# A transformer block on one core: the feed-forward computed by seven block products

## The chip, the cores and the metric

The kernel runs on one core of one Trainium2 chip. A core has five engines that work side by side, each through its own queue of instructions: TensorE (PE in the profile: matrix products, with the loading of the stationary operand shown apart as PEld), VectorE (DVE), ScalarE (ACT), GpSimd (POOL) and SyncE (SP), which here issues every DMA transfer. The engines work on SBUF, the on-chip memory of 128 partitions, and on PSUM, where products accumulate. Large data lie in DRAM and are moved by 16 DMA engines. The metric is the device time of one execution in microseconds (us). Before the change it is 2405.66 us, the median of three runs (2404.91 to 2408.99).

## The reference

One transformer block over 4096 tokens of 512 features, in fp32: linear attention, then a feed-forward, each added to its input and followed by a normalisation (eps 1e-5).

```python
x = layernorm(x + attention(x, Wq, Wk, Wv, Wo))
x = layernorm(x + ffn(x, ...))

# attention: 16 query heads, 4 key/value heads, 128 features each
q, k = elu(rope(q)) + 1, elu(rope(k)) + 1
state += k_s (x) v_s;  z += k_s                # running sums over the tokens s
out_s = (q_s . state) / (q_s . z + 1e-6)       # then out @ Wo.T

# ffn: 512 -> 2 x 2048 -> 512; fwht is the normalised Walsh-Hadamard transform
u = fwht(x * SU_ug) / 64
h = silu(u @ W_gate.T * (Wscale_ug[2048:] * 64)) * (u @ W_up.T * (Wscale_ug[:2048] * 64))
y = (fwht(h * SU_dp) / 64) @ W_down.T * (Wscale_dp * 64)
```

## The kernel before

**Precision.** Every fp32 operand of a product is split into two fp32r numbers: `hilo` (L89) copies the value to fp32r on ACT (L90), and DVE, or POOL where it is told so, subtracts the copy from the value (L91). Each product is then three matmuls: high by high, high by low and low by high.

**Attention** (L134 to L488, 0 to 941 us) runs in two halves of the heads over 16 blocks of 256 tokens: projections (`proj`, L239, 256 columns), the rotary part (POOL L221), scores, running states. It writes the unnormalised outputs to `num_d` and the reciprocals of the denominators to `rec_d`. The change leaves it as it is.

**Output projection** (L540 to L645). 32 tiles of 128 tokens. `pre` (L118) loads a tile's numerators `nt` (1 MB), its reciprocals `rb` (four loads of 256 KB, broadcast over the partitions) and its residual `xn`. `norm_o` (L549) multiplies the two on DVE (L552), one group of four heads at a time, and splits the result. 48 matmuls of 128x512 (L622) make the tile's projection in `ps_wo`; DVE adds the residual (L627), `layer_norm` (L530) takes statistics, an inverse square root of small operations (`rsqrt_small`, L32, L35 to L43) and the normalisation (L538) on DVE, and the tile goes to `y_d`.

Two more things run beside this stage. `prep_down` (L576), started at the tiles in `starts`, folds the second Walsh-Hadamard transform into the down weights: per eighth of the columns, a Hadamard matmul (L589, L590) does 7 of 11 steps, DVE scales (L591), POOL does the other four steps (L598, 64 operations of 128x512), and the split result goes to `wdn_d` in two puts of 512 KB, in runs of 256 bytes. `front` (L495) makes the first block's feed-forward input: sign product (L504), nine add/subtract steps (L509, L510), four transposes (L518) and a split; for block 0 it runs on POOL.

**Feed-forward** (L648 to L715, 1316.6 to the end). Eight blocks of 512 tokens. In each, 16 iterations `it` over 128 rows of the up and gate weights: `load_wug` (L522) loads and splits the weights, 2 x 12 matmuls of 128x512 (L682) fill `ps_gu`, ACT takes silu (L687), DVE multiplies (L688), and the product is split into `hh_h` and `hh_l`, which stay in SBUF for the block. The fronts of the next block run among the iterations, alternately on DVE and POOL. Then four tiles of 48 down matmuls (L707) with the down weights kept in SBUF since block 0, the residual (L713), the second norm and the store.

**Order.** The program is written as one sequence. A scheduler that simulates the timeline places the instructions on the engines; each engine then works through its queue in order. All DMA issues stand in SP's one queue, so a transfer that waits for data holds back the issues behind it; the transfers rotate over eight completion semaphores. A tile pool gives a buffer out again when its last reader is done.

Of the kernel before, what the change touches and what calls it, by code (L numbers as in the profile page):

```python
# [9 lines left out]
F32 = mybir.dt.float32  # L10
# [11 lines left out]
TF = 512  # L22
NF = NTOK // TF
EPS_DEN = 1e-6
EPS_LN = 1e-5
# [6 lines left out]
def rsqrt_small(nc, pool, v, tag):  # L32
    y = pool.tile([128, 1], F32, tag=tag + "y", name=tag + "y")
    a = pool.tile([128, 1], F32, tag=tag + "a", name=tag + "a")
# [3 lines left out]
    for _ in range(3):  # L38
        nc.vector.tensor_scalar(a, y, y, v, ALU.mult, ALU.mult)
        nc.vector.scalar_tensor_tensor(y, a, c, y, ALU.subtract, ALU.mult)  # L40
        f = f * -0.5 if c == 3.0 else f / (-2.0 * c / 3.0)
        c = 3.0 / (f * f)
# [5 lines left out]
def kernel(  # L48
# [28 lines left out]
    wdn_d = dram.tile([16, 128, 2, 512], F32, name="wdn_d")  # L77
# [39 lines left out]

    def pre(t):  # L118
        if t in (12, 16):
            recip(NB - 2 + (t == 16))  # L120
        nt = late["p"].tile([128, 16, 128], F32, tag="nt", name="nt", bufs=3)
        if t:
            dma(nt, num_d[t].rearrange("p g n -> p (g n)"), t < 3)
        rb = []
        for g in range(4):
            if t == 0:
                dma(nt[:, 4 * g:4 * g + 4], num_d[t][:, g])
            rb.append(late["p"].tile([128, 512], F32, tag="rb", name="rb", bufs=5))
            dma(rb[g], rec_d[t][g * 512:(g + 1) * 512].partition_broadcast(128), 0 < t < 3 and g == 0)
        xn = late["p"].tile([128, DM], F32, tag="xn", name="xn")  # L130
        dma(xn, x_n[t * 128:(t + 1) * 128])
        cur[t] = dict(nt=nt, rb=rb, xn=xn)

# [357 lines left out]
    suug = mid.tile([128, DM], F32, name="suug")  # L491
    wsc = mid.tile([128, 2, 16], F32, name="wsc")
    Y, YT = {}, {}

    def front(pool, fpool, nb, ptr, f, t, eng):  # L495
        if t == 0:
            Y[f] = []
        y = pool.tile([128, DM], F32, tag="y", name="y")
        dma(y, y_d[4 * f + t])
        Y[f].append(y)  # L500
        yield
        a = fpool.tile([128, DM], F32, tag="fw0v" if eng is V else "fw0g", name="fw0", bufs=1)
        b = fpool.tile([128, DM], F32, tag="fw1", name="fw1", bufs=nb)
        eng.tensor_tensor(a, y, suug, ALU.mult)  # L504
        w = 1
        while w < DM:
            aa = a.rearrange("p (n r w) -> p n r w", r=2, w=w)
            bb = b.rearrange("p (n r w) -> p n r w", r=2, w=w)
            eng.tensor_tensor(bb[:, :, 0], aa[:, :, 0], aa[:, :, 1], ALU.add)  # L509
            eng.tensor_tensor(bb[:, :, 1], aa[:, :, 0], aa[:, :, 1], ALU.subtract)  # L510
            a, b = b, a
            w *= 2
        yield
        if t == 0:
            YT[f] = tuple(mid.tile([128, 4, TF], F32R, tag="yT", name=n, bufs=2) for n in ("yTh", "yTl"))
        ps = ptr.tile([128, 4, 128], F32, tag="tr", name="ps_tr")
        for k in range(4):
            T.transpose(ps[:, k], a[:, k * 128:(k + 1) * 128], idt)  # L518
        h, l = (z[:, :, t * 128:(t + 1) * 128] for z in YT[f])
        hilo(h, l, ps)  # L520

    def load_wug(it):  # L522
        w = mid.tile([128, 2, 2, 4, 128], F32R, tag="wug", name="wug_s", bufs=2)
        wf = w.rearrange("p l u k m -> p l (u k m)")
        for j in range(2):
            c = slice(j * 512, (j + 1) * 512)
            hilo(wf[:, 0, c], wf[:, 1, c], load_raw(wug[it, :, c]))
        return w

    def layer_norm(pool, x, o, tag):  # L530
        bs = pool.tile([128, 6], F32, tag="bs", name="bs")
        mv = pool.tile([128, 2], F32, tag="mv", name="mv")
        vv = pool.tile([128, 1], F32, tag="vv", name="vv")
        V.bn_stats(bs, x)
        V.bn_aggr(mv, bs)
        V.tensor_scalar(vv, mv[:, 1:2], EPS_LN, None, ALU.add)
        rs = rsqrt_small(nc, pool, vv, tag)
        V.tensor_scalar(o, x, mv[:, 0:1], rs, ALU.subtract, ALU.mult)  # L538

# [1 line left out]
    with ExitStack() as es:  # L541
        p2 = es.enter_context(tc.tile_pool(name="c2", bufs=2, reuse_waits="tile"))
        p1 = es.enter_context(tc.tile_pool(name="c1", bufs=1, reuse_waits="tile"))
        pwo = es.enter_context(tc.tile_pool(name="pwo", bufs=3, space=PSUM, reuse_waits="tile"))
        pfd = es.enter_context(tc.tile_pool(name="pfd", bufs=2, space=PSUM, reuse_waits="tile"))
        ptc = es.enter_context(tc.tile_pool(name="ptc", bufs=1, space=PSUM, reuse_waits="tile"))
        pon = es.enter_context(tc.tile_pool(name="pon", bufs=2, space=PSUM, reuse_waits="tile"))

        def norm_o(t, g):  # L549
            c = cur[t]  # L550
            o32 = pon.tile([128, 4, 128], F32, tag="on", name="ps_on")
            V.tensor_tensor(o32, c["nt"][:, 4 * g:4 * g + 4], c["rb"][g].rearrange("p (h n) -> p h n", h=4), ALU.mult)  # L552
            hi, lo = (p2.tile([128, 4, 128], F32R, tag="o", name=n, bufs=10) for n in ("oh", "ol"))
# [4 lines left out]
        for h in (NH - 2, NH - 1):  # L558
            WO.append(load_w(wo[h], mid, bufs=4))
# [213 lines left out]
```

## Time and profile before

| What | us |
|---|---|
| Median of three runs (range) | 2405.66 (2404.91 to 2408.99) |
| Profiled execution, span from first to last instruction | 2408.2 |
| Attention, to the first output projection | 0 to 941.3 |
| Output projection | 941.3 to 1316.6 |
| Feed-forward, first block | 1316.6 to 1467.3 |
| Feed-forward, a later block (period) | 133.4 |
| Last operation of the tail begins | 2404.5 |

The profile gives one execution's span (first to last instruction), 2.5 us above the median of the runs. A row of a group or a timeline names start or count, duration, engine, source line, operation, the tiles written and read, and the shape (partitions x elements). Matmuls are pipelined: their shown duration (0.39 us for 512 columns) is longer than the distance from one to the next, so prices of matmuls are taken from stretches of the chain. "Granted clock" is the share of TensorE's full clock that it was given in a stretch.

### The profile page before, as it was taken

The numbers are of one execution on the slowest core, as the hardware profiler recorded it, in microseconds if no ns is written. First come the engines' busy times: TensorE is split into PE (matmuls) and PEld (weight loads), VectorE is DVE, ScalarE is ACT, GpSimd is POOL, SyncE is SP. The second block draws the span as 40 slices with busy tenths as digits, with TensorE's granted clock in tenths as the row PEclk, the third lists the DMA queues.
The fourth block names the chain that finished last, engine by engine and source line by source line (L and its number), as shares of the span: only waits on it lengthen the run. The fifth ranks groups of instructions, "written<-read, shape, count | busy, mean of one in ns | idle before, by whom it ended". The sixth has DMA issues, their size and how long they took to land.

```text
span 2408.2 us, 38221 instructions
## 1 busy us (share of the span) xinstructions
PE 2356.0 (98%) x13600; PEld 2040.2 (85%) x13600; DVE 1825.2 (76%) x3408; ACT 1106.5 (46%) x1928; POOL 848.6 (35%) x839
## 2 busy tenths in 40 slices
PE   7999999999999998999999899999999999999998
PEld 6999999999999996777888688888888888888887
DVE  6999999998888897999998847475655757475443
ACT  5777777777777774222222332314141323324140
POOL 2455454454444452684242504022220405031000
PEclk9999999999999998999999899999999999999999
DMA  6555555644554447878885532213131222223120
GB/s 181 144 157 147 176 145 151 170 132 133 140 146 137 125 135 244 285 235 274 272 275 176 177 131 76 92 60 98 44 114 59 91 70 88 83 70 95 42 92 18
DMA packets 223583, 329.97 MB, mean 137 GB/s; under 512 B 62398, under 2 KB 99328, under 8 KB 219424
## 3 DMA queue, kind: packets, MB, share of 16 engines
q1 hardware_dynamic: 223392, 327.53, 44.6%
q8 instruction: 107, 1.75, 0.3%
q14 instruction: 84, 0.69, 0.1%
HBM read 209.62 MB, written 76.02 MB: 119 GB/s over the span
## 4 chain that ended last, share of the span: by engine, by line
PE 89%; DVE 6%; DMA 2%; issue 2%; ACT 1%; POOL 0%; SPq 0%; DVEq 0%; ACTq 0%; POOLq 0%
PE ps_gu L682 28%; PE ps_qk L239 16%; PE ps_dn L707 15%; PE ps_wo L622 12%; PE ps_num L366 6%; PE ps_s L289 4%; PE ps_v L192 3%; PE ps_sc L332 1%; PE ps_den L367 1%; PE ps_sc L333 1%; DMA rb<-rec_d 1%; DVE ps_on L552 1%; PE ps_tr L518 1%; DVE fw L510 1%; PE pt L277 0%
## 5 line engine op out<-in xcount | busy, mean ns | idle before, releaser
L682 PE MATMUL ps_gu<-yTh,wug_s 128*128 128x512 f32 x2048 | 646.4, 392 | 9.8 <-DVE wug_s L91 4.1
L682 PEld LDWEIGHTS ps_gu<-yTh,wug_s 128*128 128x128 f32 x2048 | 385.8, 189 | 95.3 <-DVE wug_s L91 8.6
L682 PE MATMUL ps_gu<-yTl,wug_s 128*128 128x512 f32 x1024 | 400.6, 391 | 0.0
L239 PE MATMUL ps_qk<-xh,wh 128*128 128x256 f32 x1280 | 358.7, 280 | 5.7 <-ACT wh L90 3.9
L239 PE MATMUL ps_qk<-xl,wh 128*128 128x256 f32 x1280 | 357.0, 279 | 0.6 <-DVE xl L91 0.6
L239 PE MATMUL ps_qk<-xh,wl 128*128 128x256 f32 x1280 | 357.2, 279 | 0.0
L346 POOL TENSOR_SCALAR_AFFINE_SELECT A<-A 64x512 fp32r<-64x512 f32 x256 | 219.9, 859 | 315.5 <-DVE am L342 208.8
L707 PE MATMUL ps_dn<-wdn,hh_h 128*128 128x512 f32 x1024 | 327.9, 396 | 0.0
L688 DVE SCALAR_TENSOR_TENSOR hh<-ps_gu,wsc,sg 128x512 f32<-128x512 f32 x128 | 95.9, 749 | 269.1 <-PE ps_gu L682 267.9
L221 POOL TENSOR_TENSOR sw<-sw,csb 128x512 f32<-128x512 f32 x160 | 217.2, 1358 | 166.8 <-ACT sw L220 158.5
L90 ACT ACTIVATE wug_s<-raw 128x512 fp32r<-128x512 f32 x256 | 150.5, 626 | 230.2 <-PE ps_gu L682 192.9
L239 PEld LDWEIGHTS ps_qk<-xh,wh 128*128 128x128 f32 x1280 | 242.4, 189 | 6.9 <-ACT wh L90 4.1
L504 POOL TENSOR_TENSOR fw<-y,suug 128x512 f32<-128x512 f32 x18 | 25.1, 1393 | 633.2 <-DMA y<-y_d 603.1
L239 PEld LDWEIGHTS ps_qk<-xl,wh 128*128 128x128 f32 x1280 | 241.9, 189 | 1.8 <-DVE xl L91 0.8
L239 PEld LDWEIGHTS ps_qk<-xh,wl 128*128 128x128 f32 x1280 | 241.7, 189 | 1.1
L707 PEld LDWEIGHTS ps_dn<-wdn,hh_h 128*128 128x128 f32 x1024 | 191.6, 188 | 43.7
L682 PEld LDWEIGHTS ps_gu<-yTl,wug_s 128*128 128x128 f32 x1024 | 193.5, 189 | 40.4
L687 ACT ACTIVATE sg<-ps_gu,wsc 128x512 f32<-128x512 f32 x128 | 87.7, 686 | 264.5 <-PE ps_gu L682 264.0
L622 PE MATMUL ps_wo<-wh,ol 128*128 128x512 f32 x512 | 203.9, 398 | 1.7 <-DVE ol L91 1.7
L622 PE MATMUL ps_wo<-wh,oh 128*128 128x512 f32 x512 | 203.3, 397 | 2.2 <-ACT oh L90 2.2
L622 PE MATMUL ps_wo<-wl,oh 128*128 128x512 f32 x512 | 202.8, 396 | 0.0
L707 PE MATMUL ps_dn<-wdn,hh_l 128*128 128x512 f32 x512 | 202.1, 395 | 0.0
(122 smaller groups left out, 5116.3 us busy)
## 6 DMA issues: line engine op xcount, KB each, us to landing
raw<-in_wug_dram SPq DMA_DIRECT2D x256, 256.0 KB
vd<-vhl SPq DMA_DIRECT2D x128, 256.0 KB
num_d<-num SPq DMA_DIRECT2D x128, 256.0 KB
rb<-rec_d SPq DMA_DIRECT2D x128, 256.0 KB
nt<-num_d SPq DMA_DIRECT2D x31, 1024.0 KB
y<-y_d SPq DMA_DIRECT2D x36, 256.0 KB
raw<-in_x_t_dram SPq DMA_DIRECT2D x32, 256.0 KB
csb<-in_cs_dram SPq DMA_DIRECT2D x32, 256.0 KB
```

Source lines behind the costliest of these rows:

```text
L90: S.activation(hi, src, AF.Copy)
L192: T.matmul(ps[:, t], B[xa][:, k, t * 128:(t + 1) * 128], w[:, k % 2], start=i == 0, stop=i == 11)
L221: G.tensor_tensor(sw, sw, sinb, ALU.mult)
L239: T.matmul(ps[:, j], W[key][wa][:, k * 128:(k + 1) * 128], B[xa][:, k], start=i == 0, stop=i == 11)
L289: T.matmul(ps[:, i], B["kfn"][r, g, i // 2], B["vs"][r, i // 2, g * 128:(g + 1) * 128], start=True, stop=True)
L346: G.affine_select(ah, ah.bitcast(F32), pattern=[[0, 8], [1, 64]], compare_op=ALU.is_ge, fill=0.0, base=0, channel_multiplier=-1)
L366: T.matmul(ps[:, c2], l, r, start=i == 0, stop=i == len(ops) - 1)
L622: T.matmul(ps, l[:, h], r, start=i == 0, stop=i == 47)
L682: T.matmul(ps, w[:, wa, u, k], ya[:, k], start=i == 0, stop=i == 11)
L687: S.activation(sg, pu[0], AF.Silu, scale=wsc[:, 1, it:it + 1])
L688: V.scalar_tensor_tensor(hh, pu[1], wsc[:, 0, it:it + 1], sg, ALU.mult, ALU.mult)
L707: T.matmul(ps, l[:, ts], r, start=i == 0, stop=i == 47)
```

## The change

The feed-forward's matrix products are made by a Strassen-Winograd scheme: both operands are cut into 2 x 2 blocks, and the four result blocks come from seven block products of sums and differences of the blocks, instead of eight. `WKEY` names the seven weight operands (A11, A12, A22 and the combinations S1 to S4), `YKEY` the seven token operands (B11, B21, B22 and T1 to T4), and `SEQ` the PSUM bank in which each product is accumulated.

*Gate/up.* Four blocks f of 1024 tokens, each of two halves (even and odd tiles), and eight units p of 2 x 128 rows. A unit has 7 x 2 x 6 matmuls of 128x512. `aload` loads weight blocks of 256 KB; in block 0 `acomb` makes S1 to S4 on POOL and writes them to `was_d`, from where later blocks load them; `asplit` splits every operand of every unit. ACT copies partial sums (`sv`), DVE adds (`cc`), ACT takes silu, POOL (three of four) or DVE multiplies. The four results and POOL's four combinations of them give seven arrays that go to `hop_d` unsplit.

*Token operands.* `front` now works on pairs of tiles: four transposes per tile, the sign product on DVE, a split, a Hadamard matmul pair for seven of the nine transform steps, the other two as additions on DVE and POOL, three more combinations on POOL, and seven puts of 128 KB to `yq_d`, in runs of 512 bytes. Twelve of the sixteen pairs are made in the output projection, four in block 0. `yload` and `ysplit` bring a block's seven operands in.

*Down weights.* `prep_down` makes the seven down operands: the same Hadamard matmuls and POOL steps, 16 POOL combinations more, 28 splits, and 56 puts of 256 KB to `wdop_d`, in runs of 256 bytes (before: 16 puts of 512 KB).

*Down stage.* It stands alone at the end: 8 units x 7 products x 48 matmuls of 128x256. Every step loads its 1 MB operand from `hop_d` in four pieces, two steps ahead, and splits it again (ACT; DVE, or POOL for one or two of four). Results are added to the residual on DVE, then the second norm and the store.

*Output projection.* Two of a tile's four `norm_o` products move from DVE to POOL; the norm works on pairs of tiles, its inverse square root on two columns at once, and the normalisation itself moves from DVE to ACT; the reciprocal loads are issued one group at a time (`pre_rb`); `nt` has two buffers, not three, and the split outputs eight, not ten; the first feed-forward weights are no longer loaded there.

The diff, cut to its core:

```diff
 def rsqrt_small(nc, pool, v, tag):
...
     for _ in range(3):
-        nc.vector.tensor_scalar(a, y, y, v, ALU.mult, ALU.mult)
+        nc.vector.tensor_tensor(a, y, y, ALU.mult)
+        nc.vector.tensor_tensor(a, a, v, ALU.mult)
         nc.vector.scalar_tensor_tensor(y, a, c, y, ALU.subtract, ALU.mult)
...
+    def layer_norm(pool, xs, tag):
...
+        V.scalar_tensor_tensor(nb, mv[:, :, 0], -1.0, rs, ALU.mult, ALU.mult)
+        for j, x in enumerate(xs):
+            S.activation(x, x, AF.Identity, bias=nb[:, j:j + 1], scale=rs[:, j:j + 1])
+
+    SEQ = ("a", "c", "a", "b", "a", "a", "b")
+    WKEY = ("A11", "A12", "S2", "S1", "S3", "A22", "S4")
+    YKEY = ("B11", "B21", "T2", "T1", "T3", "T4", "B22")
+
+    def front(i, y2, spool, ptr, phd, alloc):
...
+        for e in range(2):
...
+                T.transpose(ps[:, k], y2[e][:, k * 128:(k + 1) * 128], idt)
...
+            V.tensor_tensor(ysu, ps, sut[:, :, None].to_broadcast([128, 4, 128]), ALU.mult)
...
+            hilo(hl[:, 0], hl[:, 1], ysu)
...
+            T.matmul(ps, hadr, hl[:, 0], start=True, stop=False)
+            T.matmul(ps, hadr, hl[:, 1], start=False, stop=True)
...
+            S.activation(odd, pa[:, :, 1], AF.Copy)
...
+            V.tensor_tensor(da[:, :, 0], pa[:, :, 0], odd, ALU.add)
+            V.tensor_tensor(da[:, :, 1], pa[:, :, 0], odd, ALU.subtract)
...
+        G.tensor_tensor(q[:, 0], d[:, :, 0:2], d[:, :, 2:4], ALU.add)
+        G.tensor_tensor(q[:, 1], d[:, :, 0:2], d[:, :, 2:4], ALU.subtract)
...
+            dma(yq_d[f][YKEY.index(key)][:, :, c * 128:(c + 1) * 128], x)
...
+        G.tensor_tensor(tt[:, 0], q[:, 0, 1], q[:, 0, 0], ALU.subtract)
+        G.tensor_tensor(tt[:, 1], tt[:, 0], q[:, 1, 1], ALU.subtract)
+        G.tensor_tensor(tt[:, 2], tt[:, 1], q[:, 1, 0], ALU.add)
...
         def norm_o(t, g):
...
+            if g % 2 == 0:
+                o32 = pon.tile([128, 4, 128], F32, tag="on", name="ps_on")
+                V.tensor_tensor(o32, c["nt"][:, 4 * g:4 * g + 4], rb, ALU.mult)
+            else:
+                o32 = p2.tile([128, 4, 128], F32, tag="o32", name="o32")
+                G.tensor_tensor(o32, c["nt"][:, 4 * g:4 * g + 4], rb, ALU.mult)
...
+            for key in ("B11", "B21", "B22", "T3", "T1", "T2", "T4"):
+                if key in fn:
+                    G.tensor_tensor(B[key], *fn[key])
+                x = ytile([128, 2, 8, 64], F32R, "dohl")
+                hilo(x[:, 0], x[:, 1], B[key])
+                for j in range(2):
+                    dma(wdop_d[YKEY.index(key)][j, :, :, qq * 64:(qq + 1) * 64], x[:, j])
...
+        def acomb(n, key):
...
+            G.tensor_tensor(x, r(p0), r(p1), op)
+            RAW[n, key] = x
+            dma(was_d[p][key], x.rearrange("p u k m -> p (u k m)"))
+
+        def asplit(n, s):
...
+            hilo(hi, lo, RAW[n, WKEY[s]])
...
+        for n in range(NS):
...
+            for s, tag in enumerate(SEQ):
...
                 for u in (1, 0):
...
+                    for k in range(2):
+                        for w, y in ((wh, yh), (wh, yl), (wl, yh)):
+                            T.matmul(ps, w[:, u, k], y[:, k], start=first and i == 0, stop=i == 5,
+                                     skip_group_check=not first)
...
+                    if s in (0, 2, 4):
...
+                        S.activation(x, ps, AF.Copy, scale=sc)
...
+                    if s in (1, 4, 6):
...
+                        V.scalar_tensor_tensor(x, src, sc, sv[k, u], ALU.mult, ALU.add)
+                        emit(u, q, x)
...
+                if n + 1 < NS:
+                    aprep(n + 1, s)
+                if n + 2 < NS:
+                    aload(n + 2, s)
...
+            for key, x0, x1, op in (("S1", "A21", "A22", ALU.add), ("S3", "A11", "A21", ALU.subtract),
+                                    ("S2", "S3", "A22", ALU.subtract), ("S4", "A12", "S2", ALU.add)):
+                H[key] = utile("h" + key)
+                G.tensor_tensor(H[key], H[x0], H[x1], op)
+                put(key)
...
+        def h_load(n, s):
...
+            for qd in range(4):
+                raw = pd.tile([128, 2, 256], F32, tag="hr", name="hraw", bufs=8)
+                dma(raw, hop_d[f][s, jp, :, 2 * qd:2 * qd + 2])
...
+        def h_split(n, s):
...
+                hilo(hi, lo, raw, G if qd == 1 or (qd == 3 and s % 2) else V)
...
+        for idx, (n, s) in enumerate(order):
+            if idx + 2 < len(order):
+                h_load(*order[idx + 2])
+            if idx + 1 < len(order):
+                h_split(*order[idx + 1])
...
+            for ip in range(8):
+                qd, r = divmod(ip, 2)
+                for j in range(2):
+                    js = slice(j * 128, (j + 1) * 128)
+                    for al, bl in ((0, 0), (0, 1), (1, 0)):
+                        T.matmul(ps[:, j], ops[qd][al][:, r, js], BW[s][bl][ip], start=first and i == 0, stop=i >= 45,
+                                 skip_group_check=True)
...
+            def acc(y, cols, src):
+                V.tensor_tensor(y[:, :, cols], src, y[:, :, cols], ALU.add)
...
```

## The prediction

> **What bounds the kernel now.** First the busy shares, then the chain of work that ended last:
>
> ```profile
> span 2408.2 us, 38221 instructions
> PE 2356.0 (98%) x13600; PEld 2040.2 (85%) x13600; DVE 1825.2 (76%) x3408; ACT 1106.5 (46%) x1928; POOL 848.6 (35%) x839
> ...
> PE 89%; DVE 6%; DMA 2%; issue 2%; ACT 1%; POOL 0%; SPq 0%; DVEq 0%; ACTq 0%; POOLq 0%
> ```
>
> TensorE (PE) is the bound: 98% busy, 89% of the chain. Fewer matmuls save time only if nothing else takes over, so next I cut the span into stages (columns: stretch, length, busy time of each engine, granted clock, DMA share, GB/s). The rows are attention, output projection, the first feed-forward block, the other seven up to the last down products, and the end; the last two rows are short stretches inside the output projection.
>
> ```profile
> 0.00:941.30 941.30, 910.99 (x7296) 864.26 (x7296) 836.20 (x1394) 688.61 (x1224) 448.45 (x433) 0.99 0.53 150
> 941.30:1316.60 375.30, 370.90 (x1584) 297.67 (x1585) 356.08 (x751) 97.97 (x168) 164.49 (x140) 0.99 0.81 260
> 1316.60:1467.30 150.70, 140.92 (x595) 113.17 (x594) 99.42 (x184) 42.02 (x69) 41.60 (x47) 0.94 0.41 135
> 1467.30:2357.40 890.10, 890.10 (x3944) 730.71 (x3944) 515.94 (x1023) 277.32 (x467) 194.01 (x220) 1.00 0.24 78
> ...
> 1141.00:1165.00 24.00, 24.00 (x107) 19.42 (x107) 23.47 (x60) 7.40 (x13) 1.19 (x1) 1.00 0.86 288
> 1303.00:1305.00 2.00, 2.00 (x10) 1.65 (x9) 1.96 (x8) 0.30 (x1) 0.00 (x0) 1.00 1.04 248
> ```
>
> The feed-forward has room: VectorE (DVE) 58%, GpSimd (POOL) 22%, DMA 24%. The output projection has little: DVE 95%, DMA share 0.81, PE 99%. The change puts new work into the stage with the least room, so that stage decides. Its timeline, POOL and DVE side by side, and one DVE row from the tail, where POOL rests:
>
> ```profile
> 1040.78 3.00 POOL L598 TENSOR_TENSOR dbf<-dbf 128x512 f32<-128x512 f32 x2
> ...
> 1045.12 2.99 POOL L598 TENSOR_TENSOR dbf<-dbf 128x512 f32<-128x512 f32 x2
> ```
>
> ```profile
> 1041.59 0.95 DVE L40 SCALAR_TENSOR_TENSOR r1y<-r1a,r1y 128x1 f32<-128x1 f32 x1
> ...
> 1045.10 1.86 DVE L552 TENSOR_TENSOR ps_on<-nt,rb 128x512 f32<-128x512 f32 x1
> ...
> 2403.13 0.16 DVE L40 SCALAR_TENSOR_TENSOR r2y<-r2a,r2y 128x1 f32<-128x1 f32 x1
> ```
>
> Beside POOL a one-column L40 takes 0.95 us instead of 0.16 and L552 1.86 instead of its fastest 0.68; POOL's L598 has 1.61 as its median and 1.28 as its fastest. Operations of DVE with two SBUF inputs and POOL operations get in each other's way: to first order their times add. L91 from PSUM at 1044.02 kept 0.68.
>
> Matmul prices come from the chain of one block:
>
> ```profile
> 1489.90 10.88 PE ps_gu L682 x48
> ...
> 1586.33 14.40 PE ps_dn L707 x62
> ```
>
> So 0.2267 us per gate/up matmul (512 columns) and 0.2323 per down matmul. In attention, 256-column matmuls come at 4.32 us for 38, 0.1137 each.
>
> **The change part by part.**
>
> *Attention* is not touched: 941.3.
>
> *Gate/up on PE.* 32 units x 7 products x 2 x 6 = 2688 matmuls of 512 columns in place of 3072: 696 becomes 609, 87 saved. All of it lies on the path.
>
> *Down on PE.* 2688 matmuls of 256 columns in place of 1536 of 512. At 0.1137 they take 306; at 0.120 (five 256-column ps_num of attention take 0.60) 323. I take half of 0.2323, since operands come the same way: 312, against 357. 45 saved.
>
> *Output projection.* PE: 1536 x 0.2323 = 357, 80 Hadamard matmuls x 0.23 = 18, 96 transposes x 0.12 = 12 (twelve front pairs; they were spread over the blocks before): 387. With the 4 us idle of now, 391 is the lower end. Hidden behind it must be:
> - POOL: 64 norm_o products moved from DVE, 64 L598 steps as now, 16 new weight combinations, at 1.28 each, and 12 fronts of two 512-column and three 256-column combinations (2x1.28 + 3x0.61 = 4.4): 184 + 53 = 238 us (now 131 by the same prices).
> - DVE with two SBUF inputs: 64 norm_o and 64 splits of POOL's results, 24 + 44 + 14 splits in fronts, weights and token operands, at 0.60 from start to start, 126; 144 small norm operations x 0.2 and some scalings: about 165 in all (now about 130).
> - These add up to 403, more than PE's 387. Now they are about 260 in 375, and the stage still runs at PE's rate.
> - DVE's operations from PSUM (projection adds, 64 splits, statistics, front work) are some 130 more; POOL runs beside those. Moving the normalisation to ACT costs nothing: ACT is 26% busy here.
> - DMA: per tile 2.62 MB (num_d, four rb, x, y_d), 84 MB at 335 GB/s (288 at share 0.86) = 251; 56 new weight puts in 256-byte runs, 14.7 MB at the 241 that 248 at share 1.04 comes to, 61; 84 token puts, 11 MB in 512-byte runs, of which no row exists: 33 to 46, taken 39; reads 24. Sum 375, a share of 0.9.
>
> I take 403 for the shared access plus 9 for the ends of the stage, where one engine waits for another: 412. Upper end: POOL's operations at the contended 1.61, 238x1.61/1.28 = 299, + 165 = 464, + 4 = 468. I stay near the lower end of the sum because 1.61 holds DVE's time already.
>
> The Trainium skill, page "SBUF — State Buffer", section "SBUF: two separate sides", says the shared VectorE/GpSimd port is an exclusive lock, held for the whole instruction; this speaks against moving norm_o to POOL, and this trace agrees (0.16 against 0.95). By the rule alone the stage would be 403; without it, by PE, 391.
>
> The page "DMA: Bandwidth & Descriptors", section "Specifications", wants at least 512 bytes for line rate. The trace has 241 GB/s for 256-byte writes against 335. By the rule the token puts would cost 33 of the bounds above.
>
> *Start of the feed-forward.* The first weight load stands in SP's queue behind the y_d puts of the last tile, which wait for the first norm: about 3.3 for statistics and rsqrt, 1.2 ACT, then load 3, split 1.3 and a POOL combination: 11, with a colder clock 15. The block that starts there now also loses 17 (150.7 against a period of 133.4, whose 1467.30 row runs at clock 1.00).
>
> *Block 0* (8 units). PE has four fronts more: 20.0 per unit. POOL: per unit 4 weight combinations, 3 multiplies, 4 result combinations at 1.29 and 2.2 of front: 16.4; DVE's operations with two SBUF inputs 5.5: 21.9, less a little as fronts leave units free: 21.5, so 172. Ends: 160 (PE) and 208 (16.4x1.61/1.28 + 5.5 = 26).
>
> *Blocks 1 to 3*: no weight combinations; POOL 9 + DVE 5.5 under 19.04 of PE; 24 x 19.04 x 1.02 = 466. Block boundaries with seven token loads and splits: 6. Feed-forward: 15 + 172 + 466 + 6 = 659. DMA moves 14 times 256 KB per unit, 3.7 MB in 19 us or 193 GB/s, against 335.
>
> *From feed-forward to down.* The first loads of the down stage are queued on SP behind the last result puts. After the last matmul: DVE 0.75, POOL multiply 1.3, combinations in series 3.9, put and load 3 each, split 1.3, cold start 1: 14. Now nothing of this exists, since down products run inside each block. Ends: 6 if the weights' order lets PE start early, 20 if put and load both take the 5 us of the y_d load after 1323.
>
> *Down stage.* Each step has 48 matmuls, 5.57 us. ACT four splits and a norm share, 3.2; DVE 3 to 4.5; POOL 2; DMA 1 MB plus residuals, 4. All fit; 6 us for stalls: 318.
>
> *Tail.* Two halves in pairs: 10 against 7.7.
>
> Sum: 941.3 + 412 + 659 + 14 + 318 + 10 = 2354, against the profiled span of 2408.2, which itself lies 2.5 above the median of the runs (2405.66; 2404.91 to 2408.99). Forecast 2352: 132 of matmul time is saved, 78 paid back.
>
> **The rivals.** (1 is the forecast.)
> 2. *All covered*: output projection 391, block 0 160, start 13, boundaries 0, down 306 + 4, transition 6, rest of the blocks 457: 941 + 391 + 630 + 6 + 310 + 10 - 2.5 = 2286. For it: the DVE/POOL sum exceeds PE by 4% only. Against: DVE is 95% busy there already.
> 3. *Down paced by loads*: 1.3 MB per step at 288 GB/s is 4.5, and if the split of 2 follows in series, 6.5 per step, 56 x 0.93 = 52 more: 2404, no change. Against it: two steps are loaded ahead, so load and split overlap.
> 4. *Shared access (slower)*: POOL at its contended price in the output projection, 468, and in block 0, 208: 56 + 36 = 92 more, 2444. For it: DVE loses about 4 of 8.5 us between 1040.5 and 1049 while POOL works without rest. Against: POOL has pauses and DVE's PSUM operations to run beside. It decides from 54 us of that excess on, e.g. POOL operations at about 1.47 in both places.
> 5. *256-column matmuls cost more than half*, say 0.133 as 0.28 us operations that overlap less: down saves nothing, 2398. Against: 38 of them in 4.32.
>
> **How the numbers follow.** Two executions differ by 0.2% at most as a rule, so 2400.8 to 2410.5 counts as the same. Chances: forecast 0.42 (its own range 2318 to 2395), all covered 0.18, down paced by loads 0.08, shared access 0.27, matmul price 0.05. Faster: 0.42 + 0.18 + half of 3 and 5, 0.66; same 0.06; slower 0.28. The range runs from 2286, the covered case, to 2460, the contended one with the upper ends of the down stage (323) and the transition (20) on top (11 + 6); about one in ten is left on each side.
>
> **What would show it.** Right: ps_wo lasts about 412 us with POOL near 60% busy and PE idle behind splits of o; gate/up units every 21.5 us in block 0 and 19.1 later; a single PE gap of 14 before the first down product; down matmuls 0.116 apart. Wrong: POOL's norm_o products or DVE's L40 at several times their free price over the whole stage (case 4); DMA share at 1 with PE waiting for nt or rb; PE waiting for hraw in every step (case 3); a chain of PE alone (case 2).

## The result

The changed kernel takes 2424.91 us (median of four runs, 2419.77 to 2428.04), the kernel before 2405.28 us on the same chip (2404.31 to 2408.99): a ratio of 1.0078, 95% interval 1.006 to 1.0095. It is slower by 0.8%, where 2352 us had been forecast. The page of the changed kernel, busy shares and chain:

```profile
span 2418.0 us, 42274 instructions
...
PE 2281.5 (94%) x14432; PEld 2016.3 (83%) x14432; DVE 1908.3 (79%) x3062; ACT 1354.9 (56%) x2320; POOL 1235.2 (51%) x993
...
PE 74%; DVE 12%; DMA 8%; issue 3%; ACT 2%; POOL 1%; SPq 1%; DVEq 0%; ACTq 0%; POOLq 0%
```

PE has 74 us less to do than before (2281.5 against 2356.0), but its part of the chain fell from 89% to 74%: DVE and DMA now carry a fifth of the span. The profiled execution's span is 2418.0, 6.9 below the median of the runs, so the accounts below are made from profiled execution to profiled execution. By stages (columns as before; the rows are the output projection from its first to its last matmul, the gap to the first gate/up matmul, block 0, most of blocks 1 to 3, the gap ahead of the down stage, the down stage):

```profile
939.30:1373.70 434.40, 404.56 (x1710) 319.12 (x1710) 381.91 (x645) 137.24 (x241) 251.40 (x191) 0.97 0.79 246
1373.70:1393.20 19.50, 1.42 (x4) 0.60 (x3) 13.09 (x24) 5.62 (x7) 10.62 (x8) 0.56 0.50 166
1393.20:1585.20 192.00, 172.22 (x713) 134.53 (x713) 148.87 (x160) 104.97 (x174) 149.11 (x103) 0.96 0.78 244
...
1630.90:2063.00 432.10, 431.65 (x1850) 347.05 (x1848) 277.69 (x311) 228.65 (x375) 234.95 (x156) 1.00 0.67 212
2063.00:2085.90 22.90, 0.22 (x2) 0.02 (x1) 0.75 (x1) 0.98 (x3) 6.27 (x5) 0.55 1.04 390
2085.90:2408.50 322.60, 321.71 (x2688) 321.05 (x2688) 209.66 (x468) 158.23 (x251) 106.84 (x80) 0.99 0.68 225
```

| Stretch, us | forecast | measured | difference |
|---|---|---|---|
| start to first gate/up matmul (attention, output projection, gap) | 1368.3 | 1393.2 | +24.9 |
| block 0 | 172 | 192.0 | +20.0 |
| blocks 1 to 3 | 472 | 477.6 | +5.6 |
| gap ahead of down | 14 | 22.9 | +8.9 |
| down stage | 318 | 322.6 | +4.6 |
| tail | 10 | 9.5 | -0.5 |
| sum | 2354 | 2418.0 | +64 |

In the output projection PE is idle for 30 of 434 us, and its own work is slower as well: 404.6 us busy at a granted clock of 0.97, against 391.8 at 0.99 for the same matmuls in run e9 below. What it waits for there and in the gap (waits of PE: what waited, for whom, us in total, times, longest; `yp` is a pair's projection and residual, normalised in place, `woh` the high part of a weight operand, `r1a` a scratch tile of the norm's inverse square root):

```profile
PE ps_tr L539 <- ACT yp L527: 18.4, 8, 3.7
PE ps_a L840 <- ACT woh L93: 11.9, 1, 11.9
PE ps_fd L647 <- DVE r1a L38: 6.2, 1, 6.2
```

Transposes of the fronts stand in PE's queue and wait for the normalised tile. The norm is late because of its small operations. Timeline of the changed kernel, POOL and then DVE, in the last tiles:

```profile
1382.35 2.48 POOL L658 TENSOR_TENSOR dbb<-dba 128x512 f32<-128x512 f32 x2 [26.84 <-DVE r1y L40]
1384.91 5.05 POOL L658 TENSOR_TENSOR dbb<-dbb 128x512 f32<-128x512 f32 x4
```

```profile
1376.04 0.16 DVE L38 TENSOR_TENSOR r1a<-r1y 128x2 f32<-128x2 f32 x1
...
1382.37 1.26 DVE L38 TENSOR_TENSOR r1a<-r1y 128x2 f32<-128x2 f32 x1
1383.66 1.18 DVE L39 TENSOR_TENSOR r1a<-r1a,vv 128x2 f32<-128x2 f32 x1
```

The same two-column operation takes 0.16 us while POOL rests and 1.26 beside it. A norm of a pair has 14 small operations in series, all of them on two columns.

Two prices are also to be seen in the chain, a stretch of gate/up and one of down:

```profile
1706.89 2.33 PE ps_c L840 x10
```

```profile
2127.78 5.71 PE ps_db L953 x48
```

0.2333 us per gate/up matmul where 0.2267 had been taken from the kernel before, 0.119 per down matmul where 0.116 had been.

### The profile page after: what moved, and what is told of

Read it like the earlier page. It is cut to its first block, busy times and chain, and to the rows that moved or that the text cites. A ratio compares the mean times of both kernels' runs of the same rounds, so it can differ in the third digit from the quotient of the medians.

```text
span 2418.0 us, 42274 instructions
## 1 busy us (share of the span) xinstructions
PE 2281.5 (94%) x14432; PEld 2016.3 (83%) x14432; DVE 1908.3 (79%) x3062; ACT 1354.9 (56%) x2320; POOL 1235.2 (51%) x993
## 4 chain that ended last, share of the span: by engine, by line
PE 74%; DVE 12%; DMA 8%; issue 3%; ACT 2%; POOL 1%; SPq 1%; DVEq 0%; ACTq 0%; POOLq 0%
PE ps_qk L248 15%; PE ps_a L840 12%; PE ps_da L953 8%; PE ps_wo L699 7%; PE ps_b L840 6%; PE ps_num L375 5%; PE ps_db L953 4%; PE ps_s L298 4%; PE ps_c L840 3%; PE ps_v L201 3%; PE ps_dc L953 2%; PE ps_sc L341 1%; DVE wol L94 1%; PE ps_sc L342 1%; PE ps_den L376 1%
## 5 line engine op out<-in xcount | busy, mean ns | idle before, releaser
L823 POOL TENSOR_TENSOR cc<-cc 128x512 f32<-128x512 f32 x96 | 147.9, 1542 | 248.9 <-ACT cc L820 141.9
L93 ACT ACTIVATE hah<-hraw 128x512 fp32r<-128x512 f32 x224 | 138.9, 630 | 155.1 <-PE ps_da L953 58.7
L840 PE MATMUL ps_a<-yoh,woh 128*128 128x512 f32 x512 | 203.5, 398 | 18.9 <-ACT woh L93 17.5
L94 DVE TENSOR_TENSOR wol<-S,woh 128x512 fp32r<-128x512 f32 x128 | 144.5, 1132 | 92.6 <-ACT woh L93 77.0
L94 POOL TENSOR_TENSOR hal<-hraw,hah 128x512 fp32r<-128x512 f32 x80 | 106.8, 1337 | 214.7 <-ACT hah L93 170.7
L840 PE MATMUL ps_a<-yol,woh 128*128 128x512 f32 x512 | 203.4, 397 | 0.0
L840 PE MATMUL ps_a<-yoh,wol 128*128 128x512 f32 x512 | 199.2, 396 | 1.8 <-DVE wol L94 1.8
L94 DVE TENSOR_TENSOR hal<-hraw,hah 128x512 fp32r<-128x512 f32 x144 | 106.7, 747 | 117.8 <-ACT hah L93 108.3
L847 ACT ACTIVATE sv<-ps_a,wsc 128x512 f32<-128x512 f32 x192 | 127.5, 681 | 60.3 <-PE ps_a L840 60.2
L611 POOL TENSOR_TENSOR o<-nt,rb 128x512 f32<-128x512 f32 x64 | 87.2, 1363 | 131.4 <-DVE ol L94 72.5
```

The source lines that it names most:

```text
L93: S.activation(hi, src, AF.Copy)
L94: eng.tensor_tensor(lo, src, hi.bitcast(F32), ALU.subtract)
L823: G.tensor_tensor(x, x, c.pop(("g", q)), ALU.mult)
L840: T.matmul(ps, w[:, u, k], y[:, k], start=first and i == 0, stop=i == 5, skip_group_check=not first)
L847: S.activation(x, ps, AF.Copy, scale=sc)
```

## The experiments

All ratios are to the kernel before, run beside each on the same chip. "First to last ps_wo" is the length of the output projection. A unit, below, is 84 gate/up matmuls, taken from its first matmul to the next unit's first; block 0 has eight.

| Run | median us | ratio (95%) | first to last ps_wo | block 0 |
|---|---|---|---|---|
| changed kernel | 2424.9 | 1.0078 (1.006 to 1.0095) | 434 | 192 |
| e1_norm_dve | 2402.3 | 0.9982 (0.9973 to 0.9991) | 412 | 195 |
| e2_late_fronts | 2419.7 | 1.0059 (1.0044 to 1.0074) | 429 | 194 |
| e3_few_puts | 2417.7 | 1.0051 (1.0036 to 1.0066) | 428 | 192 |
| e4_early_h | 2421.6 | 1.0071 (1.0054 to 1.0088) | 434 | 191 |
| e5_no_comb | 2417.2 | 1.0043 (1.0028 to 1.0058) | 437 | 184 |
| e6_nofwht | 2392.3 | 0.9934 (0.9917 to 0.9952) | 412 | 180 |
| e7_lncols | 2386.2 | 0.9910 (0.9893 to 0.9926) | 395 | 197 |
| e9_lncols_only | 2388.7 | 0.9926 (0.9911 to 0.9940) | 398 | 193 |
| e10_pace | 2401.1 | 0.9976 (0.9966 to 0.9985) | 421 | 181 |
| e11_bw_late | 2398.4 | 0.9965 (0.9953 to 0.9978) | 421 | 181 |
| e13_pad | 2414.7 | 1.0034 (1.0022 to 1.0046) | 434 | 189 |
| e14_before_pad | 2396.7 | 0.9959 (0.9945 to 0.9972) | | |
| e16_best | 2368.1 | 0.9840 (0.9826 to 0.9853) | 392 | 195 |
| e17_best2 | 2354.5 | 0.9778 (0.9765 to 0.9792) | 391 | 195 |

### What holds the output projection: e1, e2, e3

Theory: POOL and DVE hinder each other (shared access). Rivals: the place of the transposes in PE's queue; the DMA traffic of the puts.

```diff
 def norm_o(t, g):                                   # e1_norm_dve
-    if g % 2 == 0:
-        o32 = pon.tile(...); V.tensor_tensor(o32, c["nt"][:, 4 * g:4 * g + 4], rb, ALU.mult)
-    else:
-        o32 = p2.tile(...); G.tensor_tensor(o32, c["nt"][:, 4 * g:4 * g + 4], rb, ALU.mult)
+    o32 = pon.tile(...); V.tensor_tensor(o32, c["nt"][:, 4 * g:4 * g + 4], rb, ALU.mult)
```

> All four norm_o products of a tile go back to DVE (64 operations of 128x512 leave POOL); all else as in the changed kernel. Three theories for the output projection, which lasted 434 us from the first to the last ps_wo where PE's own work is 387. Shared access (POOL operations and DVE operations with two SBUF inputs exclude each other): POOL's share falls by 64 x 1.28 = 82 us, the sum of both from about 403 to 320, so the stage falls to 395 to 410 and the kernel by 25 to 40 us. PE's queue (transposes of the fronts stand ahead of ps_wo and wait for the norm): the waits of ps_tr for yp stay, under 10 us. DMA (the puts delay rb and nt): nothing changes in the traffic, under 5 us.

22 us less in the stage, and the kernel at 2402, 22.6 less. Shared access gave the sign; the size fell just short of it (412 for 395 to 410, 22.6 for 25 to 40), and 412 is still 21 above PE's 391, although the sum of POOL's and DVE's shared work is now 320 by the forecast's prices, far below PE's. The sum is not what sets the stage.

```diff
-        fr.append(wo_front(t // 2, [yp[:, 0], yp[:, 1]]))      # e2_late_fronts
+        fr.append((t, wo_front(t // 2, [yp[:, 0], yp[:, 1]])))
...
-    for x in list(fr):
-        step(x, 3)
+    for t0, x in list(fr):
+        if t - t0 >= 2:
+            step(x, 3)
```

> The fronts in the output projection are started two tiles later, so that their transposes come up in PE's queue about two tiles (25 us) after the last projection matmul of their pair instead of one. PE's queue theory: the waits of ps_tr for yp (18.4 us in eight places, and the colder clock after them) go, the kernel gains 15 to 30 us. Shared access: DVE is as late as before, the idle time of PE turns up as waits for oh and ol, gain under 8 us. DMA: under 5 us.

The waits of ps_tr for yp went, as PE's queue theory said, but waits of the Hadamard matmuls for fhl and others, 24.5 us together, stand in their place, and the stage is 5 us shorter. The place in PE's queue is not the cause: DVE is late, whoever waits for it.

```diff
     for j in range(2):                               # e3_few_puts
-        dma(wdop_d[...][j, ...], x[:, j])
+        if key in ("B11", "B21", "B22"): dma(wdop_d[...][j, ...], x[:, j])
```

> Four of the seven down-weight operands (T1 to T4) are made and split but not written, and the down stage reads B11's in their place: 32 of 56 puts in 256-byte runs are left out, 8.4 MB or some 35 us of DMA time; this part of the result is not computed. DMA theory: loads of rb and nt come earlier, 20 to 35 us gained in the output projection. Shared access and PE's queue: DVE, POOL and PE do the same work, within 8 us of the changed kernel.

The DMA share in the stage fell from 0.79 to 0.73 and its length by 6 us. DMA has a small part at most.

### The norm's small operations: e7, e9

```diff
-    nc.vector.tensor_tensor(a, y, y, ALU.mult)
-    nc.vector.tensor_tensor(a, a, v, ALU.mult)
+    for j in cols:                                   # one column each
+        nc.vector.tensor_scalar(a[:, j], y[:, j], y[:, j], v[:, j], ALU.mult, ALU.mult)
     nc.vector.scalar_tensor_tensor(y, a, c, y, ALU.subtract, ALU.mult)
```

The shift, the last scaling, the eps and the bias are written per column in the same way. e7_lncols is on top of e1, e9_lncols_only on top of the changed kernel.

> On top of e1_norm_dve, the norm's small operations work column by column with scalar operands, as in the kernel before, so that only three of them per pair have two SBUF tensors as inputs (before this edit nine, and the two-column scalings were held up by POOL as well). Shared access says that each held-up operation costs up to 1.2 us of latency: about 8 per pair less, 16 pairs; the norm of a pair is done 5 to 9 us earlier, the waits of ps_tr for yp (11 us) go, gain 8 to 18 us on e1_norm_dve. If the number of operations counts and not their inputs: 10 more small operations per pair, 0 to 4 us slower.

> The changed kernel with the norm's small operations column by column alone; half of norm_o stays on POOL. e1 (norm_o back on DVE) gave 22 us, the column form on top of it another 17. If the output projection is limited by the sum of POOL's work and DVE's shared work, the column form alone gives little, 0 to 8 us, since POOL's 82 us stay. If it is limited by the latency of the norm, whose small operations each wait out a POOL operation, the column form alone gives 15 to 30 us: nine held-up operations per pair become three.

16 us less than e1 in one case, 36 us less than the changed kernel in the other; the latency theory gave the right sign both times, the size in e7, and in e9 the gain is above its 15 to 30. The small operations of the changed kernel and then of e7 (all of one operation: shortest/median/longest in ns):

```profile
L38 DVE TENSOR_TENSOR r1a<-r1y x48: 149/161/1286, 970.1 to 1382.4; 128x2 f32<-128x2 f32 x48
L39 DVE TENSOR_TENSOR r1a<-r1a,vv x48: 147/161/1252, 970.8 to 1383.7; 128x2 f32<-128x2 f32 x48
```

```profile
L41 DVE TENSOR_SCALAR r1a<-r1y,vv x96: 252/266/275, 964.7 to 1344.7; 128x1 f32<-128x1 f32 x96
L42 DVE SCALAR_TENSOR_TENSOR r1y<-r1a,r1y x48: 146/161/1281, 973.4 to 1345.0; 128x2 f32<-128x2 f32 x48
```

The one-column form with scalar operands is never held up (275 ns at most here, 277 in e9), the form with two SBUF tensors is, up to 1.29 us; three per pair are left. A pair has 19 small operations in this form and not, as the expectation of e7 has it, ten more than 14. In e9 POOL does all that it does in the changed kernel:

```profile
942.20:1340.20 398.00, 391.79 (x1709) 313.11 (x1710) 357.33 (x724) 137.69 (x241) 262.76 (x191) 0.99 0.85 268
```

POOL is busy for 263 us, and the stage is 36 us shorter. So it is not POOL's load that set the stage, but how often an operation of the norm has to wait one POOL operation out. Over all 16 pairs, the rsqrt and bias operations of the first norm kept DVE for 77 us in the kernel before, 97 in the changed one and 72 in e9. Whether these 25 us count as lost time of a busy engine (DVE was busy for 333 of the 358 us from 972 to 1330 in the changed kernel) or as latency of the chain, no run tells apart; e2, where the waits only changed their place, speaks for the first. The two edits do not add up (22 and 36, together 39): with both the stage takes 395, close to PE's own 391, so little is left to gain.

### What is left, and block 0: e5, e6, e10

```diff
 def acomb(n, key):                                   # e5_no_comb
-    ...  G.tensor_tensor(x, r(p0), r(p1), op); dma(was_d[p][key], ...)
+    return                                           # aload loads a weight block instead
```

> On top of the changed kernel, S1 to S4 are not computed: a weight block is loaded in their place in every block (that part of the result is not computed), so 32 POOL operations and 32 puts leave block 0 and its loads become 7 per unit in place of 4. Block 0 took 192 us, its first three units 30.8, 25.2 and 29.8 against PE's 20. Shared access: 32 x 1.28 = 41 us less for POOL, most of it in the slow units; block 0 falls to 165 to 175. Start-up theory (first loads, token splits, the late end of the down-weight preparation): the first two units stay at 26 to 31, block 0 within 8 us of 192.

Block 0 took 184.4, just inside the start-up theory's band. The first three units went from 30.8, 25.2 and 29.8 to 27.8, 24.3 and 27.5: the weight combinations with their puts cost 7.6 us in block 0, and most of the slow start is something else.

```diff
-    for stp in range(4):                             # e6_nofwht, on e1
+    for stp in range(0):                             # and no POOL combinations
```

> On top of e1_norm_dve, prep_down leaves out its 64 POOL steps and 16 POOL combinations (the down weights are wrong; Hadamard matmuls, splits and puts stay), 102 us of POOL. Only the fronts' POOL work remains in the output projection. If the rest of the excess over PE's time (412 against 391 from first to last ps_wo) is shared access too: it falls to 388 to 396, kernel 15 to 25 us below e1_norm_dve; the small operations of the norm fall from up to 1.2 to about 0.2 us. If it is something else (load order, the norm's own latency): within 6 us of e1_norm_dve.

A miss, which mattered: the kernel is 10 us below e1, the small operations are almost free now (L38 0.21 us on average), and yet the stage stays at 412. Without POOL's steps the last Hadamard matmul of prep_down comes at 1218 us instead of 1361; its splits and puts crowd together, with a DMA share of 0.95 to 1.04 over most of the time from 1002 to 1182, and in the chain PE's stops around 1156 to 1176 come from DVE's queue, where the splits of o stand behind those of prep_down (dohl, dhl) and one wait for a put of wdop_d. Block 0, however, is 15 us shorter than in e1. That led to e10:

```diff
-    step(gd, 3)                                      # e10_pace, on e7
+    step(gd, 4)
```

> e7_lncols, with prep_down taken forward by four steps per tile in place of three, so that it ends at tile 23 and not in the last tile. Block 0's first units are 33.9, 24.6, 27.6 us there against 20 for PE. If they are slow because the end of prep_down (POOL steps, splits and puts) runs into them: units 0 to 2 fall by 10 to 20 us in sum, and the gap before the first ps_a from 16 to about 11; the output projection gets 0 to 8 us longer as the same work stands closer. If they are slow for their own work (weight combinations, token splits, fronts): within 6 us of e7_lncols.

The first part came out: units 0 to 2 take 23.3, 28.3 and 22.3 in place of 33.9, 24.6 and 27.6, and block 0 is 16 us shorter. The other two did not: the gap became 3 us longer and not 5 shorter, and the output projection 27 longer and not 0 to 8, so the kernel loses 15. Of the slow start of block 0, 12 us in these three units are the end of prep_down, and it is cheaper there than where DVE is full; the 9 us that are left above the forecast's 21.5 a unit stay open.

### The gap ahead of the down stage: e4, e11

```diff
+    if s == 1:                       # e4_early_h: after load_b(1); the scheduler issues it earlier
+        for j in range(2):
+            x = xtile([128, 2, 2, 256], F32, "hraw0")
+            for e in range(2): dma(x[:, e], hop_d[0][0, 0, :, ...])
```

> The first down step's four hraw loads are issued during the third block of the feed-forward, into buffers that stand free, and not behind the loads of the seven down-weight operands (14.7 MB) and the last puts. If it is the place in SP's queue that makes PE wait 22.7 us before the first ps_da: the gap falls to 8 to 12 us and the kernel by 10 to 14 us. If it is the volume of those loads that has to be through before anything can start, or the last result operations: within 4 us of the changed kernel.

The first down matmuls started 1 us after the last gate/up matmul, and stopped at once:

```profile
2066.01 0.51 PE L961 MATMUL ps_da<-wdo,hah 128*128 128x256 f32 x2 [0.65 <-ACT hah L93]
2087.45 0.58 PE L961 MATMUL ps_da<-wdo,hal 128*128 128x256 f32 x1 [20.93 <-DVE hal L94]
```

Gap and down stage together are 344.9 us against 345.4, so the place of these four loads in SP's queue does not make the gap. The chain behind the stop runs over loads of down weights and of yres that are queued after them; why the split `hal` of an operand that was there in time waited for them, no run shows. In the changed kernel itself the chain through the gap runs over loads too, at a DMA share of 1.04 (the row of the gap above):

```profile
2064.92 6.99 DMA wdo<-wdop_d
...
2071.93 7.03 DMA wdz<-wdop_d
...
2078.97 6.14 DMA hraw<-hop_d
```

`wdo` and `wdz` are the down weights, 14.7 MB in all, `hraw` is what the first step needs.

```diff
-    load_b(s)                        # e11_bw_late, on e10: in the last unit
+    if s < 4: load_b(s)              # 4 to 6: after the first two steps' hraw, one per step
```

> e10_pace, with the down weights of products 4 to 6 (6.3 MB of 14.7) loaded after the first two steps' hraw, each one step ahead, in SP's order fixed so. e4 showed that a first step in time is followed by a stop at the second. If the volume in front of the first steps makes the 23 us: PE's gap falls by 12 to 18 us and the first steps of the down stage get 6 to 12 us longer, 3 to 10 us gained in sum. If not: PE waits as long in the steps 4 to 6 as it gained, 0 +- 3.

Against e10 the gap fell from 21.8 to 14.2 and the down stage rose from 322.8 to 326.9; 2.6 us gained by the medians (2401.05 and 2398.43), whose ranges overlap. That is less than forecast on both counts (12 to 18 and 3 to 10) and, for the time, within the rival's 0 +- 3. What changed is the chain through the gap: down-weight loads no longer stand in it, but the last result operations (DVE 0.8, POOL 1.3 and four combinations) and the load behind them:

```profile
2047.98 2.48 POOL hS L890 x2
...
2056.49 5.94 DMA hraw<-hop_d
```

So the loads that were moved had made about 8 of the 22 us; the 14 that are left are result operations, puts and a load.

### Why a matmul of the same size has two prices: e8, e12 to e15

Without any part of the block, e8_micro runs the forms of all stages alone:

> No part of the block is computed here, only matmuls in the forms of both kernels, nothing else running: gate/up of before (stationary high and low parts in one tile, 12 per group), gate/up of the changed kernel (separate 2 KB tiles, 6 per group), the same with other tiles and group lengths, output projection (48 per group), and both down forms with 256 columns. In the kernels they come at 0.2267 (gate/up before), 0.2333 (gate/up after), 0.2323 (output projection), 0.119 (down after), 0.1137 (projections of attention). If the form makes the difference, the same prices return here, and the variants say which property it is (group length, or separate tiles). If it is where the tiles lie or what else runs: all 512-column forms at one price.

The gate/up form of the changed kernel, 96 matmuls:

```profile
41.19 21.76 PE ps_st L92 x96
```

0.2267, and the same for every 512-column form; both 256-column forms take 0.12. The form does not make the price.

> No part of the block is computed. e8 gave 0.2267 us for every 512-column form, so the 0.2333 of the changed kernel's gate/up is not its form. Here the same form runs with nothing beside it, with its token tiles at a high address as in the kernel, and beside, in turn: DVE on SBUF, DVE from PSUM, POOL, ACT from PSUM, DMA loads, and all four. If another engine or the DMA costs PE its 6.6 ns per matmul, the section beside it has 0.233 and the others 0.227; if the address does, the section with the high address; if none, it stays open.

Alone, with other token tiles, beside DVE:

```profile
41.71 21.76 PE ps_free L92 x96
63.47 21.76 PE ps_far L92 x96
...
90.67 27.20 PE ps_dve L92 x120
```

0.2267 in each section. What really ran beside them, by the windows: DVE from 91 to 117 us, POOL and ACT together from 199 to 226, DMA at a share of 0.83 from 308 to 335, and from 363 to 390 DVE, POOL and DMA (0.88) together, with ACT idle. Neighbours do not make the price. Nor does a high address as such: `ps_far` reads its tokens 20 KB further on, but that is a multiple of 512 bytes. What differs is where the operands lie to each other. In the kernels with 0.233 the addresses of the moving operand (512 or 256 columns) and the stationary one, taken in the allocator's table, which no view of the profile shows, differ by no multiple of 512 bytes (moving less stationary, modulo 512: gate/up of the changed kernel 480; output projection before 128 for 14 of 16 weight tiles); in ps_gu of before and in e8 and e12 they do.

```diff
+    mid.tile([128, 8], F32, name="pad")              # e13_pad; 32 columns in e14_before_pad
```

> The changed kernel with an unused tile of 32 bytes ahead of the token operands and all that lies behind them, so that moving and stationary operands of gate/up and of the output projection lie a multiple of 512 bytes apart; nothing else. If the place sets the price: gate/up from 0.2333 to 0.2267 per matmul, units of 19.05 us in place of 19.6 and 13 us less over the last three blocks, with block 0 and the output projection 13 to 22 us less in all. If not: units stay at 19.6 and the time within 3 us of the changed kernel.

> The kernel before with an unused tile of 128 bytes, so that the operands of its output projection and its down products lie a multiple of 512 bytes apart (gate/up already do). If the place sets the price: 0.2323 becomes 0.2267 for 3072 matmuls, 10 to 17 us faster than the kernel before. If not: the same within 3 us.

> No part of the block is computed: the gate/up form of the changed kernel alone, with the moving operand at 0, 16, 32, 64, 128, 256, 384, 480 and 512 bytes from a multiple of 512 relative to the stationary one, for 512 and then for 256 columns. If the place sets the price: 0.2267 at 0 and 512 and 0.233 at the others (or at some of them); if not, 0.2267 throughout. For 256 columns 0.12 is the price at a multiple; attention's 0.1137 would then be that of another distance.

The chain of e15, sections for 512 columns at 0, 16 and 32 bytes, then at 64 and 256:

```profile
43.90 21.76 PE ps_za L92 x96
65.66 22.24 PE ps_zb L92 x96
87.90 22.40 PE ps_zc L92 x96
```

```profile
110.30 21.97 PE ps_zd L92 x96
...
154.58 21.76 PE ps_zf L92 x96
```

and for 256 columns at 0, 32, 64 and 256 bytes:

```profile
242.89 11.51 PE ps_nza L92 x96
...
265.80 11.20 PE ps_nzc L92 x96
277.00 10.88 PE ps_nzd L92 x96
...
299.28 11.51 PE ps_nzf L92 x96
```

With 512 columns a matmul takes 0.2267 us when the two lie a multiple of 256 bytes apart and up to 0.2333 elsewhere (0.2323 at 128, 0.2332 at 480, the distances and prices of the two stages above); with 256 columns it is the other way round, 0.12 at a multiple of 256 and 0.1133 at 64. The expectation had 512 as the period and one direction; both were wrong in that. In the kernels, gate/up of e13 and the down products of e14:

```profile
1706.08 2.27 PE ps_c L841 x10
```

```profile
1577.73 14.08 PE ps_dn L708 x62
```

0.227 each. In e13 units fell from 19.6 to 19.0 us and the last three blocks by 9.5 (13 expected), block 0 by 3; the output projection, held by DVE, gained nothing, where it and block 0 should have given 13 to 22, and the down stage lost 4: by the allocator's table the same shift made its operands' distance a multiple of 256 for all tiles instead of half of them. The kernel before gains 9.5 us, 0.41%, by 128 unused bytes (10 to 17 expected). The tile that moved was the moving operand in e13 and e15 and the stationary one in e14, so it is the distance that counts and not the address of one of them.

### Together: e16, e17

> Together: norm_o on DVE, the norm's small operations column by column, the 32 bytes, and the down weights of products 4 to 6 loaded behind the first steps' hraw (prep_down at its old pace). e7_lncols gave 2386 and a ratio of 0.991; e11 gained 3 us over e10 by the loads; the pad, if the place sets the price, 13 to 22 more. Expected 2362 to 2372, ratio 0.981 to 0.986; without the effect of the place 2381 to 2386.

> e16_best, with an unused tile of 64 bytes at the head of the down stage's pool, so that moving and stationary operands of its matmuls lie 64 bytes apart (modulo 256) and not 0. If the matmul's price sets the down stage: 2688 x (0.12 - 0.1133) = 18 us less, the stage from 331 to 311 to 316, the kernel at 2348 to 2354. If loads and splits hold it at 5.7 us a step: 2364 to 2368.

e16 took 2368.07, within its range. e17 adds 64 bytes at the head of the down stage's pool:

```profile
2111.51 5.44 PE ps_db L959 x48
```

0.1133 per matmul; the down stage fell from 331.1 to 315.4 and the kernel to 2354.53, a ratio of 0.9778 (0.9765 to 0.9792), half a microsecond above the expected range. So the down stage is PE's. Against the kernel before with its own 128 unused bytes (e14, 2396.7) e17 is 1.8% faster, not 2.2%; the two ran on different chips. e17 against the changed kernel, in profiled executions, 66 us: 43.4 up to the first gate/up matmul, 8.8 in blocks 1 to 3, 10.2 in the gap, 7.2 in the down stage, less 2.5 in block 0 and 1.3 in the tail.

## Why the prediction was wrong

*Matmul counts, and that PE's savings lie on the path where PE is the bound*: right. Blocks 1 to 3 run at PE's rate, POOL, DVE and DMA hidden as forecast.

*"609, 87 saved"*: the price was mis-sized. 2688 matmuls at 0.2333 are 627, 18 us more. Of the 13 us that fell to blocks 1 to 3, the 2% laid on top of them took up 9; that these blocks were off by 5.6 only is luck. The profile of before showed both 0.2267 and 0.2323 for the same shape, and the forecast took the lower without asking what made the difference. e8, e12, e13 and e15 show that it was the distance of the operands, which the change had altered.

*"I take half of 0.2323 ... 312"*: measured 0.119, 320. The sum of 318 with its 6 us for stalls was off by 4.6 only, since hardly any stall came: luck, as two errors offset each other. By e15 the price of 256 columns isn't half of anything: it has its own dependence on the distance.

*"144 small norm operations x 0.2"* is the term that failed in the output projection. Over the 16 pairs the rsqrt and bias operations of the first norm kept DVE for 97 us, 6.1 a pair, where 29 and a little for scalings had been taken, although the quoted row of before had L40 at 0.95. They were counted into a sum of shared work (403); but e1 lowered that sum to 320 and left 412, and e9 left POOL's work where it was and reached 398. What counts is how often a small operation waits for a POOL operation, on an engine whose queue also feeds PE. The diff showed the cause, two tensor_tensor on two columns in place of one tensor_scalar with scalar operands on one column, and the forecast read it as two short operations.

The Trainium skill, page "SBUF — State Buffer", section "SBUF: two separate sides", names this: a DVE operation with two SBUF inputs blocks for a whole GpSimd operation. The rows agree (0.16 against 1.26 us; 0.277 at most for the form with scalars). The forecast used the rule for the sum of times; e9 shows that it has to be used for each small operation, one wait apiece.

*Rival 4, shared access,* named the mechanism and the stage, and its sign came (L40 0.52 us on average, 0.16 free). It priced it with POOL's contended 1.61; POOL's operations were less slow (L611 1.37, L658 1.46 on average) and POOL had pauses, while DVE's small operations took three times their free price. Its sum had 56 us more in the output projection and 36 in block 0; 22 and 20 came, the latter in the first three units alone.

*Start, "with a colder clock 15"*: 19.5 from the last ps_wo. *Block 0, "172"*: 192. The sum of POOL's and DVE's work holds from the fourth unit on (20.3 to 22.0 for 21.5); the first three take 21 us more, of which 12 are the end of prep_down, which the forecast had ended with the output projection (e10 moved 16 us out of block 0 and paid 27 for it). The other 9 stay open.

*"From feed-forward to down ... 14"*: 22.9, since the sum left out the loads of the seven down operands, 14.7 MB, which come in the last unit. e4 speaks against the order on SP; in e11, with 6.3 MB of them out of the way, the chain is the one that the forecast had added up, and the gap 14.2.

One reading of the DMA sum is off without effect: 248 at a share of 1.04 comes to 238 GB/s and not 241, under 1 us more for the puts.

## What to carry to other kernels

Next to a busy GpSimd, write short dependent VectorE operations so that they read one SBUF tensor of one column and scalars: here 19 operations per pair in place of 14 cost less than the waits that they saved. Don't price an engine's short operations by their free duration when the row beside a busy neighbour is on the same page, and where equal instructions have two prices, ask for the cause before taking either. Try a few unused bytes between pools whose tiles meet in a matmul: here that was worth 0.4% for the kernel before, and 0.6% for the last version.

## What the runs showed of the hardware

A matmul's distance to the next depends on the distance in SBUF between its moving and its stationary operand, with opposite preference for 512 and 256 columns: 0.2267 to 0.2333 us and 0.1133 to 0.12 us. Why is not shown. How a scaling with a constant fares beside POOL depends on the width of its tile: on two columns L43 took 0.48 us on average, on one column in the kernel before 0.149. And a cheaper neighbour is not always a gain: without POOL's steps (e6), or with them taken earlier (e10), the splits and puts behind them came at a time when DVE and DMA had no room.
